# Statistics in larger pieces, a gather moved behind a projection, and a product moved between two others, in an attention and scan kernel

## The chip, the cores and the metric

The kernel runs on one core of a Trainium2 chip. The time is that of one launch on the device, in microseconds (us); the smaller the better. The core has five engines that run side by side, each with its own queue of instructions, worked off in order: TensorE (PE in the profile) multiplies matrices, VectorE (DVE), ScalarE (ACT) and GpSimd (POOL) work on rows of numbers in 128 partitions, and SyncE (SP) issues the DMA transfers between the chip's main memory and the on-chip memory. TensorE writes its results to PSUM, which has eight banks; a bank is 512 float32 numbers in each partition. Everything here is float32.

## The reference

The input x has two images of 256 x 256 positions with 128 channels. Two layers are computed, each added to its input.

```python
x = x + attention(_gn(x))      # layer 0
x = x + scan(_gn(x))           # layer 1
```

`_gn` is a group norm: the 128 channels fall into 32 groups of 4, and every group of an image is brought to mean 0 and variance 1 over all its 65,536 x 4 numbers. So a layer can begin with an image only when the statistics of that whole image are there.

The attention projects each position to q, k, v1, v2 (128 x 128 weights), takes for every position (i, l) the softmax over j of q[i, l] . k[l, j], averages v2 with it, multiplies with v1 and projects once more.

The scan layer is a state space model over the positions of an image in row order:

```python
xi, z = split(x @ in_proj_w.T)                  # 256 channels each
xi = silu(depthwise_conv_3x3(xi) + conv_b)
dts, Bs, Cs = split(x_proj_w @ xi)              # 8, 16 and 16 rows
delta = softplus(dt_w @ dts + dt_b)
h = exp(delta * A) * h + (delta * xi) * B       # step by step, 256 channels x 16 states
y = sum(h * C) + Ds * xi
y = layernorm(y) * ln_g + ln_b
out = (y * silu(z)) @ out_proj_w.T
```

## The kernel before

**Preparation and the first statistics.** Line 72 and the lines after it load weights and biases, all through the sync queue. Lines 150 to 157 bring `A_logs` into order with 32 tiny transfers. Lines 168 to 195 turn the weights with TensorE, and each of the nine convolution taps is multiplied into the input projection (VectorE, line 185), so that projection and convolution become nine matmuls. Behind them `piece_stats` (line 246) reads image 1 in NT = 16 pieces of 128 x 32 positions into six buffers and has VectorE take `bn_stats` of each of the 32 groups: 128 numbers (32 positions x 4 channels) in each partition, six numbers out. `group_stats` (line 204) then makes the scale `rs` and shift `sh` of every channel: 32 `bn_aggr` on VectorE, each over the six numbers of every piece; a matmul with a matrix of 1/128 (`ones_mean`) for the mean over partitions; small VectorE operations; two more matmuls that bring the group's values to its channels; and a power of -1/2 on GpSimd. This part has no order written out by hand; the framework places it by its own costs, in the order of the program where nothing else speaks.

**Attention** (lines 278 to 575). 256 calls of two columns each, in an order written out by hand for TensorE, ScalarE, VectorE and GpSimd. The statistics of image 2 for layer 0 (`image_load`, `image_stats`, lines 491 to 501) and those of both images for layer 1 (`column_stats`, line 483) are spread over the calls, six pieces a call. `gather` (line 486) is `group_stats` on them. Image 2's layer-1 gather is the very last thing, since the attention's last columns belong to it.

**The scan stage** (from line 577). Its buffers take over the memory of the attention's, and so its first loads wait until the attention's last user of that memory is done. An image has 64 steps of four rows (1024 positions); there are 128 steps. A step has 32 units: 8 groups of 32 channels by 4 groups of 4 states. For a unit `decay` (ScalarE, line 958) writes exp(delta A) into one of two PSUM buffers, `drive` (GpSimd, line 968) makes delta xi B for two units at a time, `scan` (VectorE, line 980) runs the recurrence, and `product` multiplies with C: on VectorE (line 995) for 21 units of a step, on GpSimd (lines 995 and 1004) for 11. `remember` (ScalarE, line 985) keeps the last state. `add_up` (TensorE, line 1027) sums four units' products; a product's buffer is free again when that is done.

Beside the units run three chains that feed them and finish them. `project(k)` (line 623) prepares step k: it loads rows (`load`), turns and normalises them (`turn`, `normalise`), and runs the convolution matmuls (`conv`), the gate's matmuls (`gate`), and those for B, C and delta (`states`, `size`). Each of these writes one PSUM bank, the pool `ps_p` with a single buffer, and ScalarE empties it before the next may be written. `finish_row` (line 813) takes a finished row: `turn` and `stats`, the layer norm (`scales`, `norm`), `back` (the transposes into `yd`, line 865), `gated` (VectorE, line 873: yd times silu(z)), `mix` and `leave`. Its bank is `ps_f`, also a single buffer.

The order is written out by hand again, in slots: slot t holds unit t, and `at(t, piece)` puts a piece of the chains into slot t. `project(k)` begins 72 slots ahead of its step, so slots -84 to -1 hold nothing but the projections of steps 0, 1 and 2. A row's `gated` lies in the slots with t mod 8 = 5, so in units 5, 13, 21 and 29 of a step. In a slot the loop at line 1054 emits, for each engine in this order: fetch, drive, GpSimd's products, decay of unit t + 1, `scan(t)`, `product(t)`, the pieces that `at` put there, first those that aren't TensorE's, then TensorE's, `add_up`, and `remember(t)`:

```python
            if 0 <= t < end:
                scan(t)
                if not pooled(t):
                    product(t)
            others, on_pe = slots.pop(t, ((), ()))
            for piece, args in others:
                piece(*args)
```

Of the kernel before, what the change touches and what calls it, by code (L numbers as in the profile page):

```python
# [8 lines left out]
F32 = mybir.dt.float32  # L9
# [12 lines left out]
def attn_then_ssm_kernel(  # L22
# [46 lines left out]
    def column(name, src):  # L69

        t = const.tile([P, 1], F32, name=name)
        nc.sync.dma_start(out=t, in_=src.rearrange("(p o) -> p o", o=1))
        return t
# [9 lines left out]
    ones_mean = const0.tile([P, P], F32, name="ones_mean")  # L83
    nc.vector.memset(ones_mean, 1.0 / P)
# [4 lines left out]


# [9 lines left out]
    bq_c = column("bq_c", bq)  # L100
    bv1_c = column("bv1_c", bv1)
# [102 lines left out]
    def group_stats(stats, pool, psum, name, tag="mm"):  # L204


        mv = pool.tile([P, G, 2], F32, name="mv")
        for g in range(G):
            nc.vector.bn_aggr(mv[:, g, :], stats[:, g, :, :])
        gm_ps = psum.tile([P, G], F32, name="gm_ps", tag=tag)  # L210
        nc.tensor.matmul(gm_ps, ones_mean, mv[:, :, 0], start=True, stop=True)
        gm = pool.tile([P, G], F32, name="gm")
        nc.vector.tensor_copy(gm, gm_ps)
        dev = pool.tile([P, G], F32, name="dev")
        nc.vector.tensor_tensor(dev, mv[:, :, 0], gm, ALU.subtract)
        dev2 = pool.tile([P, G], F32, name="dev2")
        nc.vector.tensor_tensor(dev2, dev, dev, ALU.mult)
        pv = pool.tile([P, G], F32, name="pv")
        nc.vector.tensor_tensor(pv, dev2, mv[:, :, 1], ALU.add)
        ex = pool.tile([P, 2, G, CG], F32, name="ex")  # L220
        nc.vector.tensor_copy(ex[:, 0], gm.unsqueeze(2).to_broadcast([P, G, CG]))
        nc.vector.tensor_copy(ex[:, 1], pv.unsqueeze(2).to_broadcast([P, G, CG]))
        cs_ps = psum.tile([P, 2], F32, name="cs_ps", tag=tag)
        for i in range(2):
            nc.tensor.matmul(
                cs_ps[:, i : i + 1],
                ex[:, i].rearrange("p g c -> p (g c)"),
                ones_mean[:, 0:1],
                start=True,
                stop=True,  # L230
            )
        cs = pool.tile([P, 2], F32, name="cs")
        nc.vector.tensor_copy(cs, cs_ps)
        ve = pool.tile([P, 1], F32, name="ve")
        nc.vector.tensor_scalar(ve, cs[:, 1:2], GN_EPS, None, ALU.add)
        rs = const.tile([P, 1], F32, name=f"rs_{name}")
        nc.gpsimd.tensor_tensor(rs, ve, neg_half[:, 0:1], ALU.pow)
        sh = const.tile([P, 1], F32, name=f"sh_{name}")
        nc.vector.tensor_scalar(sh, cs[:, 0:1], rs, -1.0, ALU.mult, ALU.mult)
        return rs, sh  # L240

    gn0 = {}
    TT = 32
    NT = L // (P * TT)

    def piece_stats(b, k, stats, pool):

        xt = pool.tile([P, TT, C], F32, name="xt")
        nc.sync.dma_start(
            out=xt,  # L250
            in_=x_tok[b, k * P * TT : (k + 1) * P * TT, :].rearrange("(p t) c -> p t c", p=P),
        )
        for g in range(G):
            nc.vector.bn_stats(stats[:, g, k, :], xt[:, :, g * CG : (g + 1) * CG])

    with tc.tile_pool(name="st", bufs=1) as stp, tc.tile_pool(
        name="st_x", bufs=6
    ) as stx, tc.tile_pool(name="st_ps", bufs=2, space=PSUM) as st_ps:
        stats = stp.tile([P, G, NT, 6], F32, name="stats")
        for k in range(NT):  # L260
            piece_stats(0, k, stats, stx)
        gn0[0] = group_stats(stats, stp, st_ps, "0_0")

# [13 lines left out]
    gn1 = {}  # L277
    with ExitStack() as actx:
# [207 lines left out]
        def gather(to, b, stats, layer):  # L486
            to[b] = group_stats(stats, ap1, ps, f"{layer}_{b}", "t0")
# [119 lines left out]
    slots = {}  # L607

# [13 lines left out]

    def project(k):
# [6 lines left out]
        o = {}  # L630

# [24 lines left out]
        def turn(src, r, m):  # L656
            t_ps = o["t"] = ps_p.tile([P, RB, W], F32, name="t_ps", tag="p")
            for i in range(m):
                for t in range(WT):
                    nc.tensor.transpose(  # L660
                        t_ps[:, i, t * P : (t + 1) * P], o[src][:, r + i, t, :], ident
                    )
# [10 lines left out]
        def conv(h, i, taps):  # L673
            if taps[0] == 0:
                o["u"] = ps_p.tile([P, RB, W], F32, name="u_ps", tag="p")
# [26 lines left out]
        def gate(h, i):  # L702
            o["z"] = ps_p.tile([P, RB, W], F32, name="z_ps", tag="p")
# [21 lines left out]
        def states(i):  # L725
            o["xd_ps"] = ps_p.tile([64, TB], F32, name="xd_ps", tag="p")
# [17 lines left out]
        def size(h, i):  # L744
            o["dt"] = ps_p.tile([P, TB], F32, name="dt_ps", tag="p")
# [67 lines left out]
    def finish_row(k, b, row, t0, a):  # L813
# [84 lines left out]
        for i, piece in (  # L898
# [5 lines left out]
            (5, gated),  # L904
# [3 lines left out]
            at(a + i, piece, pe=piece in (turn, back, mix))  # L908

# [41 lines left out]
    def pooled(t):  # L951
        return t % NU - t % 2 in POOLED or t % NU == SINGLE
# [100 lines left out]
    with tc.manual_schedule(engines=engines):  # L1053
        for t in range(min(slots), max(slots) + 1):
# [14 lines left out]
            if 0 <= t < end:  # L1069
                scan(t)  # L1070
                if not pooled(t):
                    product(t)
# [50 lines left out]
```

## Time and profile before

| | us |
|---|---|
| time, median of 3 runs (15882.23 to 15885.26) | 15883.89 |
| the profiled execution's own time | 15886.66 |
| its span, first to last instruction | 15884.8 |
| `bn_stats` of image 1 begin | 41.55 |
| `sh` of image 1, layer 0, begins | 158.81 |
| last `bn_aggr` group of the attention begins | 2523.20 |
| first scan begins | 2675.52 |

Busy over the whole span: VectorE 14454.8 us (91%), TensorE 13780.9 (87%), GpSimd 13328.8 (84%), ScalarE 10796.7 (68%). The rows of the profile name an instruction by line, engine, operation, and tiles as output<-inputs, with sizes as partitions x elements; x16 is a count. In a timeline a row is the start, the duration, and then in brackets how long the engine had been idle and what ended that. In a table of groups a row has the busy time and the mean duration in ns, and behind the bar the idle time before such instructions and what ended most of it. PEclk, or the column behind GpSimd's in a table of stretches, is the clock that TensorE was granted, 1.00 being full. Neighbouring VectorE instructions can overlap by some ns in these records.

### The profile page before, as it was taken

The page shows a single profiled execution, that of the slowest core. Times are in us where ns is not written, and L with a number is a line of the kernel's source. Part 1 is how long each engine was busy: PE and PEld are TensorE (multiplying, and loading weights), DVE is VectorE, ACT ScalarE, POOL GpSimd, SP SyncE. Part 2 cuts the span into 40 slices and gives each one's busy share as a digit, 9 for nine tenths or more (in the row PEclk, how much of TensorE's full clock was granted, in tenths as well). Part 3 has the DMA queues.
Part 4 walks back from the last instruction along what each step waited for, and adds up shares of the span by engine and source line. Part 5 has one row for each costly group of instructions (what it writes and reads, how often), then busy time and mean ns, then how long its engine had stood idle before and what let it go on. Part 6 is the DMA issues. An engine that isn't in the chain of part 4 may idle for free. (4 is left out here: it accounts for less than half of the span.)

```text
span 15884.8 us, 178043 instructions
## 1 busy us (share of the span) xinstructions
PE 13780.9 (87%) x59451; PEld 7002.8 (44%) x59451; DVE 14454.8 (91%) x12356; ACT 10796.7 (68%) x20003; POOL 13328.8 (84%) x3344
## 2 busy tenths in 40 slices
PE   6999998888888888888888888888888888888886
PEld 4877884333333333333333333333333333333333
DVE  7665555999999999999999999999999999999998
ACT  3555554777777777777777677777777777777775
POOL 1111113999999999999999999999999999999998
PEclk8999998999999999999999999999999999999998
DMA  4322222767677767677777667777677767776675
GB/s 188 123 101 86 80 96 105 239 238 245 240 241 242 246 240 240 240 245 241 243 242 244 230 241 242 242 244 244 240 241 241 245 241 243 242 244 240 240 243 185
DMA packets 1428908, 3452.13 MB, mean 217 GB/s; under 512 B 119785, under 2 KB 711185, under 8 KB 1407505
## 3 DMA queue, kind: packets, MB, share of 16 engines
q1 hardware_dynamic: 1427984, 3440.73, 62.6%
q8 instruction: 468, 7.67, 0.2%
q14 instruction: 456, 3.73, 0.1%
HBM read 2752.41 MB, written 687.88 MB: 217 GB/s over the span
## 5 line engine op out<-in xcount | busy, mean ns | idle before, releaser
L968 POOL TENSOR_TENSOR hb<-du_r,bb 128x2048 f32<-128x2048 f32 x2048 | 9243.5, 4545 | 82.3 <-DMA du_r<-du_d 15.7
L980 DVE TENSOR_TENSOR_SCAN da<-da,state,hb 128x1024 f32<-128x1024 f32 x2688 | 6300.4, 2344 | 137.9 <-ACT da L958 134.3
L958 ACT ACTIVATE da<-delta_r,a_neg 128x1024 f32<-128x1024 f32 x4096 | 4580.7, 1118 | 88.9 <-DMA delta_r<-delta_d 10.1
L678 PE MATMUL u_ps<-xn,w_tap 128*128 128x512 f32 x9216 | 4335.3, 612 | 91.3 <-ACT sz L715 73.2
L995 DVE TENSOR_TENSOR yc<-da,cc 128x1024 f32<-128x1024 f32 x2688 | 3291.8, 1225 | 235.9 <-PE y L1027 69.1
L980 DVE TENSOR_TENSOR_SCAN hb<-da,state,hb 128x1024 f32<-128x1024 f32 x1408 | 3233.4, 2334 | 61.5 <-ACT state L985 47.7
L1004 POOL TENSOR_TENSOR yc<-hb,cc 128x2048 f32<-128x2048 f32 x640 | 2909.0, 4545 | 101.0 <-ACT state L985 81.1
L678 PEld LDWEIGHTS u_ps<-xn,w_tap 128*128 128x128 f32 x9216 | 1713.7, 195 | 2453.6 <-issue 1837.9
L1027 PE MATMUL y<-yc,sel 128*32 128x512 f32 x16384 | 2323.6, 689 | 18.5 <-POOL yc L1004 18.1
L435 POOL TENSOR_TENSOR x1g<-xc,bo_all 128x512 f32<-128x512 f32 x256 | 316.0, 1276 | 1840.5 <-DVE stats L484 1839.6
L985 ACT COPY state<-da 128x1 f32<-128x1 f32 x2688 | 425.9, 158 | 1637.5 <-DVE yc L995 1630.1
L830 PE MATMUL yt<-centre,ys 128*128 128x256 f32 x4096 | 1030.9, 395 | 284.7 <-ACT ob L891 284.7
L1027 PEld LDWEIGHTS y<-yc,sel 128*32 128x32 f32 x16384 | 470.2, 121 | 1790.0 <-issue 1646.5
L704 PE MATMUL z_ps<-xn,w_z 128*128 128x512 f32 x1024 | 696.3, 768 | 547.0 <-ACT xn L665 307.3
L746 PE MATMUL dt_ps<-xd,w_dt 8*128 8x512 f32 x1024 | 740.6, 811 | 482.0 <-ACT delta L757 385.6
L385 ACT ACTIVATE e<-s_ps,nmx 128x256 f32<-128x256 f32 x1024 | 477.6, 476 | 967.7 <-DVE nmx L376 960.0
L985 ACT COPY state<-hb 128x1 f32<-128x1 f32 x1408 | 268.5, 191 | 1242.7 <-DVE hb L980 1242.6
L830 PEld LDWEIGHTS yt<-centre,ys 128*128 128x128 f32 x4096 | 742.0, 191 | 464.4 <-ACT ob L891 381.9
L881 PE MATMUL o_ps<-w_out,szr 128*128 128x128 f32 x4096 | 793.9, 276 | 0.0
L881 PE MATMUL o_ps<-w_out,yg 128*128 128x128 f32 x4096 | 792.8, 275 | 0.0
L352 DVE TENSOR_TENSOR v<-v_ps,bv_all 128x512 f32<-128x512 f32 x256 | 177.1, 692 | 592.1 <-PE v_ps L345 592.1
L775 POOL TENSOR_TENSOR xs<-delta,xs 128x1024 f32<-128x1024 f32 x256 | 606.7, 2370 | 99.1 <-ACT delta L765 99.1
(134 smaller groups left out, 17280.7 us busy)
## 6 DMA issues: line engine op xcount, KB each, us to landing
bb<-bc_d SPq DMA_DIRECT2D x1024, 512.0 KB, 4.0
cc<-bc_d SPq DMA_DIRECT2D x1024, 512.0 KB, 5.3
delta_r<-delta_d SPq DMA_DIRECT2D x1024, 512.0 KB, 6.3
du_r<-du_d SPq DMA_DIRECT2D x1024, 512.0 KB, 5.2
sz_d<-sz SPq DMA_DIRECT2D x128, 1024.0 KB, 6.5
szr<-sz_d SPq DMA_DIRECT2D x512, 256.0 KB, 4.1
xs_d<-xs SPq DMA_DIRECT2D x128, 1024.0 KB, 9.5
xr<-xs_d SPq DMA_DIRECT2D x256, 512.0 KB, 5.9
```

Of the source, the lines that this page charges most:

```text
L678: nc.tensor.matmul(o["u"], w_tap[:, h, tap, :], xn[:, i * RB + dy : i * RB + dy + RB, dx : dx + W], start=(tap == 0), stop=(tap == 8),)
L704: nc.tensor.matmul(o["z"], w_z[:, h, :], xn[:, 1 + i * RB : 1 + (i + 1) * RB, 1 : W + 1], start=True, stop=True,)
L746: nc.tensor.matmul(o["dt"], w_dt[:, h, :], o["xd"][0:DR, i * TB : (i + 1) * TB], start=True, stop=True,)
L830: nc.tensor.matmul(o["yt"][:, j, :], ys[k, h][:, t0 + j * P : t0 + (j + 1) * P], centre[:, (1 - h) * P : (1 - h) * P + DI], start=(h == 0) ...
L881: nc.tensor.matmul(o["o"][:, j, :], o[by][:, h, j * P : (j + 1) * P], w_out[:, i, h, :], start=False, stop=(j == WT - 1 and h == NH - 1 an ...
L958: nc.scalar.activation(da, spreads["delta", k, h, q], AF.Exp, scale=a_neg[:, g, m : m + 1])
L968: nc.gpsimd.tensor_tensor(hb, spreads["pair", k, h, q], repeats["bb", k, h, m].unsqueeze(1).to_broadcast([P, 2, T]), ALU.mult,)
L980: nc.vector.tensor_tensor_scan(u["h"], u["da"], u["hb"], st, ALU.mult, ALU.add)
L985: nc.scalar.copy(st, units[t]["h"][:, T - 1 : T])
L995: eng.tensor_tensor(u["yc"], u["h"], repeats["cc", k, h, m], ALU.mult)
L1004: nc.gpsimd.tensor_tensor(yc, hb, repeats["cc", k, h, m].unsqueeze(1).to_broadcast([P, 2, T]), ALU.mult)
L1027: nc.tensor.matmul(y[q * CQ : (q + 1) * CQ, cols], sel, units[t + q]["yc"][:, cols], start=False, stop=(m == NSG - 1),)
```

## The change

- Image 1's layer-0 statistics are taken in 8 pieces of 128 x 64 positions in place of 16 of 128 x 32. A piece comes in two transfers of the old size, into three buffers in place of six; there are 256 `bn_stats` of 256 numbers, and each `bn_aggr` reads 8 x 6 numbers. The first two pieces, with their transfers, are put ahead of the weights in the program; the other six stay behind the preparation.
- `group_stats` is cut in two: `group_means` (the 32 `bn_aggr`) and `group_scales`, which gives two pieces, `means` and `scales`. The matrix `ones_mean` goes; the matmuls use columns of `centre`, which hold -1/256, and the copies out of PSUM become multiplications with -2. The small tiles become slices of one.
- For image 2 and layer 1 the attention's end runs `group_means` only. `means` goes into slot -2 of the scan stage and `scales` into slot -1.
- In `project(0)`, and there alone, the tiles go to the banks of `ps_f` and `ps_p` in turn.
- `gated` is emitted between `scan(t)` and `product(t)` of its slot, no longer behind the product. The slots are the same.
- Some small constants move from one pool to another.

```diff
+    TT0 = 2 * TT
+    NT0 = NT // 2
+    def piece_stats(b, k, stats, pool):
+        xt = pool.tile([P, TT0, C], F32, name="xt")
+        src = x_tok[b, k * P * TT0 : (k + 1) * P * TT0, :].rearrange("(p t) c -> p t c", p=P)
+        for t in range(0, TT0, TT):
+            nc.sync.dma_start(out=xt[:, t : t + TT], in_=src[:, t : t + TT])
+        for g in range(G):
+            nc.vector.bn_stats(stats[:, g, k, :], xt[:, :, g * CG : (g + 1) * CG])
+    first = ExitStack()
+    stp = first.enter_context(tc.tile_pool(name="st", bufs=1))
+    stx = first.enter_context(tc.tile_pool(name="st_x", bufs=3))
+    stats = stp.tile([P, G, NT0, 6], F32, name="stats")
+    for k in range(2):
+        piece_stats(0, k, stats, stx)
...
+    def group_means(stats, pool):
         mv = pool.tile([P, G, 2], F32, name="mv")
         for g in range(G):
             nc.vector.bn_aggr(mv[:, g, :], stats[:, g, :, :])
+        return mv
+    def group_scales(mv, pool, psum, name, tag="mm", work="gw"):
+        keep = const0 if name[0] == "0" else const
+        rs = keep.tile([P, 1], F32, name=f"rs_{name}")
+        sh = keep.tile([P, 1], F32, name=f"sh_{name}")
+        MEAN = -DI / P
+        o = {}
+        def means():
+            gm_ps = psum.tile([P, G], F32, name="gm_ps", tag=tag)
+            nc.tensor.matmul(gm_ps, centre[:, 0:P], mv[:, :, 0], start=True, stop=True)
+            w = o["w"] = pool.tile([P, 2, 2 * P], F32, name=work)
+            gm, dev, dev2, pv = (w[:, 1, i * G : (i + 1) * G] for i in range(4))
+            nc.vector.tensor_scalar(gm, gm_ps, MEAN, None, ALU.mult)
...
+            nc.vector.tensor_copy(ex[:, 1], pv.unsqueeze(2).to_broadcast([P, G, CG]))
+        def scales():
+            cs_ps = psum.tile([P, 2], F32, name="cs_ps", tag=tag)
+            for i in range(2):
+                nc.tensor.matmul(
+                    cs_ps[:, i : i + 1],
+                    o["ex"][:, i].rearrange("p g c -> p (g c)"),
+                    centre[:, 0:1],
+                    start=True,
+                    stop=True,
+                )
...
+            nc.gpsimd.tensor_tensor(rs, ve, neg_half[:, 0:1], ALU.pow)
+            nc.vector.tensor_scalar(sh, cs[:, 0:1], rs, -1.0, ALU.mult, ALU.mult)
+        return (rs, sh), (means, scales)
...
     with tc.tile_pool(name="st_ps", bufs=2, space=PSUM) as st_ps:
-        for k in range(NT):
+        for k in range(2, NT0):
             piece_stats(0, k, stats, stx)
         gn0[0] = group_stats(stats, stp, st_ps, "0_0")
+    first.close()
...
         def gather(to, b, stats, layer):
-            to[b] = group_stats(stats, ap1, ps, f"{layer}_{b}", "t0")
+            if (layer, b) == (1, B - 1):
+                last.append(group_means(stats, const))
+            else:
+                to[b] = group_stats(stats, ap1, ps, f"{layer}_{b}", "t0")
...
+    gn1[B - 1], pieces = group_scales(last[0], s1, ps_f, f"1_{B - 1}", "f", "yn")
+    for i, piece in enumerate(pieces):
+        at(i - 2, piece)
...
+        def bank(shape, name):
+            o["n"] = o.get("n", 0) + (k == 0)
+            pool, tag = ((ps_p, "p"), (ps_f, "f"))[o["n"] % 2]
+            return pool.tile(shape, F32, name=name, tag=tag)
...
-            t_ps = o["t"] = ps_p.tile([P, RB, W], F32, name="t_ps", tag="p")
+            t_ps = o["t"] = bank([P, RB, W], "t_ps")
...
             (4, back),
-            (5, gated),
             (7, mix),
             (8, leave),
         ):
             at(a + i, piece, pe=piece in (turn, back, mix))
+        between[a + 5] = gated
...
             if 0 <= t < end:
                 scan(t)
+            if t in between:
+                between[t]()
+            if 0 <= t < end:
                 if not pooled(t):
                     product(t)
```

The tiles `u_ps`, `z_ps`, `xd_ps` and `dt_ps` of `project` change to `bank` as `t_ps` does.

## The prediction

> **What bounds the kernel now.** I read the timeline of the first 160 us, the sync queue's waits there, the timeline round 2500 us, VectorE's groups in the scan stage, and single scan steps with the clock that TensorE was granted. Times are us from the span's start.
>
> ```profile
> 8.73 20.60 SPq L152 DMA_DIRECT2D alog_d<-in_L_conv_A_logs_dram  x32
> 32.41 71.57 SPq L249 DMA_DIRECT2D xt<-in_x_dram  x16
> 41.55 99.29 DVE L254 BATCH_NORM_STATS2 stats<-xt 128x6 f32<-128x128 f32 x512 [0.15 <-issue]
> 140.73 14.44 DVE L209 BATCH_NORM_AGGREGATE mv<-stats 128x2 f32<-128x96 f32 x32
> 158.81 0.21 DVE L239 TENSOR_SCALAR sh<-cs,rs 128x1 f32<-128x1 f32 x1 [0.73 <-POOL rs L237]
> ```
>
> Until 158.81 nothing but statistics ends late: the sync queue issues weights up to 32.41, 32 tiny transfers (0.64 each) among them; then VectorE alone works, 512 x 194 ns and 32 x 451 ns. The queue's waits:
>
> ```profile
> SPq L142 <- DMA bo_all<-in_L_conv_bo_dram: 0.2, 1, 0.2
> SPq L145 <- DMA cb_c<-in_L_conv_conv_b_dram: 0.2, 1, 0.2
> ```
>
> Each names the transfer eight places before it: no more than eight are under way.
>
> ```profile
> 2523.20 14.43 DVE L209 BATCH_NORM_AGGREGATE mv<-stats 128x2 f32<-128x96 f32 x32
> 2541.54 0.21 DVE L239 TENSOR_SCALAR sh<-cs,rs 128x1 f32<-128x1 f32 x1 [0.66 <-POOL rs L237]
> 2541.89 0.36 SPq L635 DMA_DIRECT2D raw<-x  x1
> ```
>
> ```profile
> 2669.83 9.86 PE L678 MATMUL u_ps<-xn,w_tap 128*128 128x512 f32 x18 [0.68 <-ACT sz L715]
> ...
> 2675.52 2.36 DVE L980 TENSOR_TENSOR_SCAN da<-da,state,hb 128x1024 f32<-128x1024 f32 x1 [133.76 <-ACT da L958]
> ```
>
> Image 2's gather lies bare (2523.20 to 2541.75), and only then may the scan stage load into the freed memory. From 2546.6 to 2675.52 TensorE and ScalarE take turns on one PSUM bank.
>
> ```profile
> L980 DVE TENSOR_TENSOR_SCAN da<-da,state,hb 128x1024 f32<-128x1024 f32 x2350 | 5508.1, 2344 | 3.8 <-POOL state L1059 3.3 <-ACT da L958 0.5
> L995 DVE TENSOR_TENSOR yc<-da,cc 128x1024 f32<-128x1024 f32 x2350 | 2877.8, 1225 | 205.3 <-PE y L1027 59.6 <-DVE da L980 1.4 <-issue 0.4
> L980 DVE TENSOR_TENSOR_SCAN hb<-da,state,hb 128x1024 f32<-128x1024 f32 x1230 | 2824.7, 2334 | 55.6 <-ACT state L985 42.0 <-ACT da L958 13.2 <-issue 0.2
> L873 DVE TENSOR_TENSOR yg<-yd,szr 128x512 f32<-128x512 f32 x447 | 304.3, 681 | 0.0
> ```
>
> From 2675.52 on VectorE is the bound: 11,515 us busy in a window of 11,500 (neighbours overlap). The idle time before L995 is partly a dependence: a product, which reads what the scan wrote, starts 34 ns or more after the scan's recorded end; independent neighbours start 83 ns before it. One step (32 units, from 5756.70 to 5859.11: 102.41) shows the rest. Windows (TensorE, weights, VectorE, ScalarE, GpSimd busy, then clock), then unit 13, then unit 28:
>
> ```profile
> 5796.82:5800.23 3.41, 3.41 (x11) 0.92 (x4) 3.32 (x3) 3.38 (x3) 3.33 (x3) 0.50 0.91 317
> 5800.23:5803.65 3.42, 3.42 (x13) 1.69 (x12) 3.39 (x3) 3.33 (x6) 3.42 (x1) 1.00 1.03 379
> 5844.61:5848.02 3.41, 3.21 (x10) 0.90 (x14) 3.41 (x2) 3.10 (x8) 3.41 (x2) 0.50 0.93 301
> 5848.02:5851.43 3.41, 3.41 (x17) 1.17 (x10) 3.10 (x3) 3.38 (x3) 3.41 (x2) 1.00 0.64 245
> ```
>
> ```profile
> 5799.62 2.35 DVE L980 TENSOR_TENSOR_SCAN da<-da,state,hb 128x1024 f32<-128x1024 f32 x1
> 5802.00 1.23 DVE L995 TENSOR_TENSOR yc<-da,cc 128x1024 f32<-128x1024 f32 x1
> 5803.14 0.68 DVE L873 TENSOR_TENSOR yg<-yd,szr 128x512 f32<-128x512 f32 x1
> 5803.74 4.58 DVE L980 TENSOR_TENSOR_SCAN hb<-da,state,hb 128x1024 f32<-128x1024 f32 x2
> ```
>
> ```profile
> 5801.91 0.60 PE L865 MATMUL yd<-ident,yn 128*128 128x128 f32 x4
> ```
>
> ```profile
> 5849.35 1.22 DVE L995 TENSOR_TENSOR yc<-da,cc 128x1024 f32<-128x1024 f32 x1 [0.31 <-PE y L1027]
> ```
>
> The clock is halved in stretches of 3.4, 6.8 or 10.2 us. Unit 28's product waits 0.31, of it 0.22 for TensorE's sums, which ran at half clock until 5848.02. Most steps take 102.40 to 102.46, 30 x 3.413.
>
> The Trainium skill ("TensorE: Matmul & The Clock Gate", "Part 1: The HAM clock gate") says that this gate judges activity in free-running windows of 3413 ns. The stretches agree; by the rule a step tied to the gate can only take whole windows, and a VectorE saving below one window would be worth nothing.
>
> **The change, part by part.**
>
> *First statistics.* Eight pieces of 64 tokens instead of sixteen of 32: 256 bn_stats of 256 elements. No row has that length; it costs between 194 ns (no growth) and 388 (double). VectorE's products of 1024 start the next instruction 1141 ns later, the gate products of 512 598: 1.06 ns an element and 54 fixed, which gives 190 at 128 (194 measured) and 326 at 256. I take 326: 10.4 a piece. bn_aggr reads 48 numbers instead of 96: between 225 and 451 ns; with the same fixed part 253, so 8.1 instead of 14.4.
>
> Four transfers of 2.1 MB now lead the queue. Before, the first such one landed 7.9 after its issue (40.31), the next 4.85 apart; from 0.73 on that is 8.6, 13.5, 18.3 and 23.2. The transfers in places 9 to 12 wait for these. The twelfth, lng_c, leaves at 23.2 instead of 4.10: all behind it moves by 19.1, the tiny transfers included, and the third piece leaves at 32.41 + 19.1 = 51.5 and has landed at 64.3. Weight preparation (32.0 to 41.5 before) ends at 60.6, hidden there. VectorE does pieces one and two meanwhile and stands idle; six pieces follow without a gap, since a piece lands in 9.7: 64.3 + 62.6 = 126.9, not 140.84. With 8.1 and the unchanged 3.8 of the scale chain, sh is there at 138.9 instead of 159.02. Late next: the attention's second load, issued behind the last bn_stats, lands 12.7 later (139.6) and costs about 0.9; the first statistics piece of image 2, queued behind it, lands at 144.5, and VectorE, in order, reaches v2 0.9 late. Front: 20.1 - 0.9 - 0.9 = 18.3 gained. Ends: 3 (bn_stats of pieces one and two queued behind the preparation) and 43 (the third piece's transfers ahead of the weights, VectorE never idle).
>
> *Image 2's gather.* The 32 bn_aggr stay; the chain behind them (2537.63 to 2541.75) leaves this place: loads start 4.1 earlier.
>
> *Two banks in the first projection.* TensorE's waits for the bank there were 0.70, 0.87, 0.96, three of 0.78 and four of 0.68 up to 2589.56: 7.6. Later ones, beside the second projection, were 0.67, 0.67 and four of 0.78: 4.5. At the border between the two (2598.33) ScalarE's copies keep 0.6 of 0.78. Sum 12.2, if every one goes. If the clock then stays full in the two convolutions that took 9.7 and 9.8 instead of 7.99, 3.5 more; taken as 0.
>
> *The moved chain.* It sits in slots -2 and -1, ahead of the first scan on VectorE, and its first matmul stands behind 16 of 18 matmuls of the third projection's first convolution: 2669.83 + 16/18 x 9.86 = 2678.6. From matmul to sh the chain took 4.0; with the last tap between, 4.3. GpSimd's pow queues behind one drive product, already done. The first scan would be at 2682.9; less 4.1 and 12.2, 2666.6 instead of 2675.52: 8.9 gained of 16.3. VectorE being the bound, it holds to the end.
>
> *Gate product inside* (four a step). Between scan and product it fills the dependence: 34 + 83 = 117 ns saved. In units 5 and 29 the transposes yd are done 3.3 and 0.24 before the new start. In unit 21 the gain is lost: the next scan waits 0.375 for ScalarE's decay anyway. In unit 13 yd ends at 5802.51, while the scan lets go at 5799.62 + 2.26 = 5801.88: VectorE waits 0.67, and the next scan starts 0.55 later than 5803.74. Its decays keep 0.6 us of slack or more. The product, which waited for nothing, now queues behind that wait.
>
> What settles it is the phase to the clock windows. After a late step the trace shows unit 28's wait falling 1.19, 0.71, 0.47, 0.35 with steps of 103.36, 102.89, 102.64, 102.52: the wait shrinks by half of any drift, until the step is 102.40. VectorE's saving of 3 x 0.117 = 0.35 must then reappear in unit 28: 0.22 + 0.35 = 0.57. At that phase yd comes early: in the steps with waits of 0.71 and 0.47 it ended 1.73 and 1.49 after scan 13's start, before 2.26. So unit 13 costs nothing, and neither is anything gained: 102.40 again. I take 0 for the 128 steps. The ends: 45 gained (128 x 0.35, no tie to the clock) and 49 lost.
>
> [...]
>
> Sum: 18.3 + 8.9 + 0 = 27.2. The profiled execution took 15886.66 (span 15884.8), 2.8 over the median of 15883.89; off the median, **15856.7**.
>
> **Rivals.**
> 1. *Slower: unit 13's wait becomes VectorE's limit.* Two steps with waits of 0.46 show yd at 3.13, where others of 0.47 have 1.49: there the wait jumps. With units shifted by 0.12 the jump is at 0.52; the tie holds if the gates save over 0.30 together. Below that each round passes the jump, some 6.5 steps a window instead of 16: (3.41/6.5 - 3.41/16) x 128 = 40 lost; without feedback (0.55 - 0.12 - 0.05) x 128 = 49. It decides from 27.2/128 = 0.21 a step. 15897 to 15906.
> 2. *The gates bring their time*, if the scan stage isn't tied: 45 more, 15812. Against: 102.40 to 102.46 in most steps.
> 3. *The front gains nothing*: VectorE holds the first pieces behind the preparation: 3 instead of 18, 15872. For it: the queue's order delays all weights.
>
> **Numbers.** Forecast 0.53, rivals 0.21, 0.08, 0.18. A measurement tells about 0.2% (31.8) from no change. The forecast's own range is 15840 to 15874 (bn_stats 0.30 to 0.36; 3.5 of clock; whole windows of 3.4), so 0.4 of it is beyond 0.2%: faster 0.21 + 0.08 + 0.02 from rival 3 = 0.31; slower 0.08 from rival 1 and 0.02 from others; same 0.59. Range: leaving out rival 2 and the upper end of rival 1, 15828 to 15902.
>
> **What would show it.** bn_stats of about 0.33 in two groups with a gap before 64; sh near 139; the first scan near 2648 (2675.5 - 18.3 - 8.9); steps of 102.4 with a wait near 0.57 at unit 28 and none before the gate product of unit 13. Wrong if steps average over 102.9 or under 102.4, or if the third piece lands far from 64.

## The result and the profile after

The changed kernel took 15842.3 us (median of nine runs, 15839.0 to 15846.1) against 15883.5: a ratio of 0.9974, interval 0.9966 to 0.9982, so 41 us gained where 27.2 were forecast. Its profiled execution has a span of 15840.8 against 15884.8, 44.0 less. All times below are us.

Where the 44.0 lie, read off at four marks of the two traces:

| mark | before | after | gained up to here | forecast |
|---|---|---|---|---|
| image 2's last bn_aggr begin | 2523.20 | 2505.61 | 17.6 | 18.3 |
| first scan | 2675.52 | 2638.52 | 37.0 | 27.2 |
| last scan ends | 15829.57 | 15786.43 | 43.1 | 27.2 |
| span | 15884.8 | 15840.8 | 44.0 | 27.2 |

The start, VectorE's timeline (start, duration, engine, line, operation, tiles; in brackets the idle time before it and what ended that):

```profile
13.21 21.03 DVE L103 BATCH_NORM_STATS2 stats<-xt 128x6 f32<-128x256 f32 x64 [11.29 <-DMA xt<-in_x_dram]
...
63.22 62.87 DVE L103 BATCH_NORM_STATS2 stats<-xt 128x6 f32<-128x256 f32 x192 [3.29 <-DMA xt<-in_x_dram]
126.01 7.48 DVE L230 BATCH_NORM_AGGREGATE mv<-stats 128x2 f32<-128x48 f32 x32
...
137.12 0.21 DVE L269 TENSOR_SCALAR sh<-gw,rs 128x1 f32<-128x1 f32 x1 [0.67 <-POOL rs L268]
```

192 bn_stats in 62.87 are 327 ns each (forecast 326); they end at 126.0 (126.9), bn_aggr takes 7.5 (8.1), sh is there at 137.3 (138.9). The sync queue shows what the third piece still waits for:

```profile
0.73 1.92 SPq L101 DMA_DIRECT2D xt<-in_x_dram  x4
...
27.14 20.60 SPq L173 DMA_DIRECT2D alog_d<-in_L_conv_A_logs_dram  x32
...
50.82 44.99 SPq L101 DMA_DIRECT2D xt<-in_x_dram  x12
```

Round 2500 the chain behind the 32 bn_aggr is gone from its old place, and TensorE starts at 2524.84 instead of 2546.63. Its timeline from there:

```profile
2525.29 2.02 PE L697 MATMUL t_ps<-ident,raw 128*128 128x128 f32 x8
2527.31 1.50 PE L741 MATMUL z_ps<-xn,w_z 128*128 128x512 f32 x2
2528.65 23.34 PE L715 MATMUL u_ps<-xn,w_tap 128*128 128x512 f32 x54
2551.83 2.93 PE L741 MATMUL z_ps<-xn,w_z 128*128 128x512 f32 x6
...
2626.13 9.31 PE L715 MATMUL u_ps<-xn,w_tap 128*128 128x512 f32 x16 [0.68 <-ACT sz L752]
2635.28 0.30 PE L244 MATMUL gm_ps<-mv,centre 128*128 128x32 f32 x2
```

In the first projection there is no wait left, and three convolutions take 23.34 in one run, where the first alone took 11.06 before. The matmul gm_ps of the moved chain stands behind 16 of the 18 matmuls, as forecast.

In the scan stage nearly every step still takes 102.40. A regular step shows the two places that the forecast was about, unit 13 and unit 28 (VectorE's timeline of step 23):

```profile
5039.04 2.35 DVE L1017 TENSOR_TENSOR_SCAN da<-da,state,hb 128x1024 f32<-128x1024 f32 x1
5041.30 0.67 DVE L910 TENSOR_TENSOR yg<-yd,szr 128x512 f32<-128x512 f32 x1
5041.89 1.21 DVE L1032 TENSOR_TENSOR yc<-da,cc 128x1024 f32<-128x1024 f32 x1
...
5089.05 1.22 DVE L1032 TENSOR_TENSOR yc<-da,cc 128x1024 f32<-128x1024 f32 x1 [0.72 <-PE y L1064]
```

Unit 13's gate product starts 2.26 after its scan, without a wait. What the gate products save reappears at unit 28: 0.72 of idle time, 0.31 before.

The exceptions are seven steps of 104.5, each followed by 103.2 and 102.65 to 102.8; before there were eight steps of 103.9 to 104.6. Each such train, a slip in what follows, adds up to one clock window (3.4) over steps of 102.40. One of them, step 24, at units 8, 13 and 28:

```profile
5124.93 2.33 DVE L1017 TENSOR_TENSOR_SCAN da<-da,state,hb 128x1024 f32<-128x1024 f32 x1
5127.70 1.23 DVE L1032 TENSOR_TENSOR yc<-da,cc 128x1024 f32<-128x1024 f32 x1 [0.44 <-DVE da L1017]
...
5144.89 0.69 DVE L910 TENSOR_TENSOR yg<-yd,szr 128x512 f32<-128x512 f32 x1 [0.75 <-PE yd L902]
...
5193.38 1.23 DVE L1032 TENSOR_TENSOR yc<-da,cc 128x1024 f32<-128x1024 f32 x1 [1.45 <-PE y L1064]
```

Unit 8's product starts 0.44 after the scan whose data it reads, where 0.09 is usual. It waits for no other engine. This stall of 0.352 delays a product once in 16 steps, in the kernel before too (there at units 12 and 18), and it had no place in the forecast. Much of what follows is about it. Six of the seven slips begin with it, and seven of the eight before. The remaining slip of each begins elsewhere: ScalarE waits for the transfer that brings `delta_r`, here in step 14 of the kernel before and in step 39 of the changed one; no run shows why it lands late just there.

```profile
4121.02 1.12 ACT L958 ACTIVATE da<-delta_r,a_neg 128x1024 f32<-128x1024 f32 x1 [1.74 <-DMA delta_r<-delta_d]
...
6647.29 1.12 ACT L995 ACTIVATE da<-delta_r,a_neg 128x1024 f32<-128x1024 f32 x1 [1.26 <-DMA delta_r<-delta_d]
```

### The profile page after: what moved, and what is told of

It reads as the page before. It is cut to its first block, busy times and chain, and to the rows that moved or that the text cites. A ratio compares the mean times of both kernels' runs of the same rounds, so it can differ in the third digit from the quotient of the medians.

```text
span 15840.8 us, 177783 instructions
## 1 busy us (share of the span) xinstructions
PE 13760.4 (87%) x59451; PEld 6981.7 (44%) x59451; DVE 14380.1 (91%) x12099; ACT 10833.2 (68%) x20003; POOL 13334.4 (84%) x3344
## 5 line engine op out<-in xcount | busy, mean ns | idle before, releaser
L715 PE MATMUL u_ps<-xn,w_tap 128*128 128x512 f32 x9216 | 4239.5, 601 | 37.1 <-ACT sz L752 33.4
L1032 DVE TENSOR_TENSOR yc<-da,cc 128x1024 f32<-128x1024 f32 x2688 | 3285.2, 1222 | 255.7 <-PE y L1064 104.9
L715 PEld LDWEIGHTS u_ps<-xn,w_tap 128*128 128x128 f32 x9216 | 1675.0, 191 | 2326.8 <-issue 1873.3
L1064 PE MATMUL y<-yc,sel 128*32 128x512 f32 x16384 | 2415.4, 713 | 18.5 <-POOL yc L1041 17.7
L741 PE MATMUL z_ps<-xn,w_z 128*128 128x512 f32 x1024 | 738.4, 812 | 626.4 <-ACT xn L702 313.8
L783 PE MATMUL dt_ps<-xd,w_dt 8*128 8x512 f32 x1024 | 696.8, 766 | 507.1 <-ACT delta L794 415.1
L918 PEld LDWEIGHTS o_ps<-w_out,yg 128*128 128x128 f32 x4096 | 664.9, 193 | 27.1
```

The costliest lines, as they stand in the source:

```text
L715: nc.tensor.matmul(o["u"], w_tap[:, h, tap, :], xn[:, i * RB + dy : i * RB + dy + RB, dx : dx + W], start=(tap == 0), stop=(tap == 8),)
L741: nc.tensor.matmul(o["z"], w_z[:, h, :], xn[:, 1 + i * RB : 1 + (i + 1) * RB, 1 : W + 1], start=True, stop=True,)
L783: nc.tensor.matmul(o["dt"], w_dt[:, h, :], o["xd"][0:DR, i * TB : (i + 1) * TB], start=True, stop=True,)
L918: nc.tensor.matmul(o["o"][:, j, :], o[by][:, h, j * P : (j + 1) * P], w_out[:, i, h, :], start=False, stop=(j == WT - 1 and h == NH - 1 an ...
L1032: eng.tensor_tensor(u["yc"], u["h"], repeats["cc", k, h, m], ALU.mult)
L1064: nc.tensor.matmul(y[q * CQ : (q + 1) * CQ, cols], sel, units[t + q]["yc"][:, cols], start=False, stop=(m == NSG - 1),)
```

## The experiments

Each was timed beside the kernel before, whose median was 15885 to 15888 in these comparisons; gains against it are taken within each. Gains against the changed kernel are taken against its 15842.3, and carry those 3 us or so. First one part of the change at a time.

**Gate products alone.** On the kernel before:

```diff
             if 0 <= t < end:
                 scan(t)
+            if t in between:
+                between[t]()
+            if 0 <= t < end:
                 if not pooled(t):
                     product(t)
```

> The kernel before with the gate product issued between a unit's scan and its product, and nothing else. Theory (tie): the 0.35 us a step that VectorE saves come back as a longer wait of unit 28's product (0.31 of idle before it becomes about 0.7), steps stay at 102.4, and the time stays within 7 us of 15883.5, that is 15877 to 15887, with a step or two more or less of 3.4 us. Rival 1 (gates bring their time): 128 x 0.35 = 45 less, 15838, steps of 102.05. Rival 2 (unit 13's gate product waits 0.67 in every step and is the limit): 40 to 49 more, 15923 to 15932.

15857.0, 29.5 less than 15886.5 (ratio 0.9983, 0.9974 to 0.9992): none of the three. The tie itself held: the median step is 102.40 and unit 28's idle time 0.71. What went is the slips: one of eight is left, and that one (step 94) begins with `delta_r`, 1.10 late, not with a stall. The stall is still there, in the same steps and at the same units 12 and 18. Step 37, first of the kernel before (TensorE's sums, then the products of units 12 and 28), then the same two products with the gate products alone:

```profile
6511.52 3.64 PE L1027 MATMUL y<-yc,sel 128*32 128x512 f32 x16
...
6515.65 1.23 DVE L995 TENSOR_TENSOR yc<-da,cc 128x1024 f32<-128x1024 f32 x1 [0.46 <-PE y L1027]
...
6567.66 1.23 DVE L995 TENSOR_TENSOR yc<-da,cc 128x1024 f32<-128x1024 f32 x1 [1.45 <-PE y L1027]
```

```profile
6502.90 1.23 DVE L996 TENSOR_TENSOR yc<-da,cc 128x1024 f32<-128x1024 f32 x1 [0.44 <-issue]
...
6553.87 1.22 DVE L996 TENSOR_TENSOR yc<-da,cc 128x1024 f32<-128x1024 f32 x1 [0.55 <-PE y L1028]
```

The first product's row names TensorE, but the sums end at 6515.16, half a microsecond before it starts. With 0.31 of spare time at unit 28 a stall of 0.35 made the sums so late that the step lost a window; with 0.71 it only shortens the wait to 0.55. So here the gate products bring no shorter step, but a margin.

**Larger pieces alone.** The changed kernel with its other three parts undone, cut to the lines that put them back:

```diff
-            pool, tag = ((ps_p, "p"), (ps_f, "f"))[o["n"] % 2]
+            pool, tag = (ps_p, "p")
...
-            if (layer, b) == (1, B - 1):
-                last.append(group_means(stats, const))
-            else:
-                to[b] = group_stats(stats, ap1, ps, f"{layer}_{b}", "t0")
+            to[b] = group_stats(stats, ap1, ps, f"{layer}_{b}", "t0")
...
+            (5, gated),
...
-        between[a + 5] = gated
```

> The changed kernel with the gate products, the banks and the second image's gather put back as before: the first statistics in larger pieces are what is left of the change. The prediction's term was 18.3, the trace of the changed kernel has 17.6 at the start of image 2's last bn_aggr (2523.20 against 2505.61): 15883.5 - 17.6 = 15866, give or take one clock window of 3.4. Rival (the attention stage hides part of it, as the prediction's third rival had it): 3 less, 15880.

15852.7, 33.8 less (0.9981, 0.9972 to 0.9990). Up to image 2's bn_aggr 18.0 are gained, as read from the traces, and 1.7 more on the way to the first scan; but the scan stage is 14.2 shorter too (13139.8 against 13154.1), though nothing in it was edited. There are four slips instead of eight: the stall now falls on unit 0 in the first image (three times, a slip each time; the fourth slip begins with a late `delta_r`) and on unit 20 in the second. At unit 20 it costs nothing: in that step the wait of 0.375 at unit 22, for ScalarE, is gone instead.

**Two banks alone.** On the kernel before, the function `bank` of the change, used for all tiles of the projections.

> The kernel before with the first projection's tiles alternating between the two PSUM banks, and nothing else. The prediction's term was 12.2, the bank waits alone: 15871. Rival, read from the trace of the changed kernel: from TensorE's first transpose to the third projection's first convolution it took 101.3 instead of 123.2, 21.9 less: 15862, with the convolutions of the first projection at 7.8 each instead of 11.1, 8.0, 8.0 and 8.0, since the clock stays full and the matmuls' own latency no longer lies between them.

15866.2, 20.4 less (0.9988, 0.9979 to 0.9997). In the trace the first scan is at 2652.63, 22.9 earlier, of which 1.1 is already there at TensorE's first transpose: 21.8, the rival's reading. The scan stage takes exactly as long as before, 13154.05 in both.

The three alone sum to 83.7, and the change with all three brings 41. The parts are at odds somewhere, and most of it lies in the scan stage: gates and pieces alone shorten it by 29.5 and 14.2, the whole change by 6.1. A smaller rest lies ahead of it: the first scan comes 2.8, 19.7 and 22.9 earlier in the three, 45.3 in sum, and 37.0 with the whole change. The gather moved behind the projection is in that 37.0, and was not run alone.

**Where the stall falls.** Counting VectorE's instructions in the traces, those that only handle semaphores included, every stall that I saw sits at a number that leaves 63 when divided by 128: 6079, 7487, 8895 and 10303 in the kernel before, 6847 and 12095 with the larger pieces alone. A step has 88 instructions, and 16 steps are 11 times 128. The reverse does not hold. Of the eleven such numbers in 16 steps of the kernel before (first image) three show the stall: the product of unit 12 and two semaphore instructions, at units 3 and 23, which start 0.35 late within a wait that ends no later for it. At the other eight nothing starts late. The change leaves VectorE 253 instructions fewer, all ahead of the scans, and that shifts the stall. So five idle instructions more, and nothing else:

```diff
     nc.vector.memset(neg_half, -0.5)
+    spare = const.tile([P, 1], F32, name="spare")
+    for _ in range(5):
+        nc.vector.memset(spare, 0.0)
```

> The changed kernel with five more VectorE instructions (memsets of 128x1, 0.06 us each) at the very start, where VectorE waits 11 us for data anyway; nothing else. Theory (place of the stall): VectorE stalls 0.352 us once in 16 steps, always at an instruction whose number in its stream, semaphore instructions counted, leaves 63 when divided by 128; a step is 88 instructions, so the stall's place in the step repeats every 16 steps and depends on the number of instructions ahead, modulo 8. Before and the kernel with the gates alone have 253 more instructions ahead than the changed kernel; 253 is 5 modulo 8. With five more the stall moves from units 8 and 0 (where it made unit 13 wait 0.75 and cost a clock window of 3.4 us each time) to units 12 and 18 (where unit 28's spare 0.6 takes it up, as in the kernel with the gates alone): six or seven slips fewer, 20 to 25 less than 15842, 15817 to 15824. Rival (the slips have another cause, and five idle memsets do nothing): 15842 give or take 4.

15816.7 (0.9958, 0.9945 to 0.9970): 25.7 less than the changed kernel, by five instructions that do nothing. The stall sits at units 12 and 18, and none of the seven slips is left. Units 12 and 28 of step 34:

```profile
6159.00 1.23 DVE L1035 TENSOR_TENSOR yc<-da,cc 128x1024 f32<-128x1024 f32 x1 [0.44 <-issue]
...
6209.97 1.23 DVE L1035 TENSOR_TENSOR yc<-da,cc 128x1024 f32<-128x1024 f32 x1 [0.57 <-PE y L1067]
```

**Why units 8 and 0 are bad places.** By the trace of step 24 the stall delays what TensorE does next so that unit 13's transposes come late, which the gate product inside now waits for. TensorE in step 23, without a stall, and in step 24; below, the table of stretches for the matmuls ahead of the transposes (busy time of TensorE, weights, VectorE, ScalarE and GpSimd, then the clock):

```profile
5037.35 2.84 PE L715 MATMUL u_ps<-xn,w_tap 128*128 128x512 f32 x6
5040.03 0.60 PE L902 MATMUL yd<-ident,yn 128*128 128x128 f32 x4
...
5140.45 3.96 PE L715 MATMUL u_ps<-xn,w_tap 128*128 128x512 f32 x6
5144.25 0.60 PE L902 MATMUL yd<-ident,yn 128*128 128x128 f32 x4
```

```profile
5037.00:5040.00 3.00, 3.00 (x10) 1.19 (x7) 2.91 (x3) 2.97 (x3) 2.92 (x2) 1.00 0.95 296
5140.00:5144.00 4.00, 4.00 (x10) 1.70 (x7) 3.91 (x3) 3.97 (x3) 3.92 (x2) 0.66 1.04 296
```

The half clock lasts 6.83 in step 23 and ends at 5036.93; in step 24 it lasts one window more, 10.24, and ends only at 5142.74. So a stall of 0.35 makes the transposes 1.83 later, counted from the step's start. The first attempt to take that wait away was a misreading:

> The changed kernel with one order changed on TensorE: in slot 12 of a step the four transposes yd, which unit 13's gate product needs, are issued ahead of three matmuls of a convolution instead of behind them, so yd is ready 1.3 to 2.5 us earlier. Theory: the stall at units 8 and 0 stays where it is, but unit 13 no longer turns it into a wait of 0.75, unit 28's spare time takes it up, and the slips of 3.4 us go: 20 to 25 less than the changed kernel, 15817 to 15824, steps still 102.40. Rival (unit 13 plays no part, the late sums alone cause the slips): 15842 give or take 4.

15843.6 (0.9973), the changed kernel's time. The edit changed nothing in TensorE's order: a tap of an f32 convolution is two matmul instructions, so the six that stood ahead of the transposes were the three taps of slot 11, not of slot 12. The run is a repetition of the changed kernel. The right edit issues the transposes a slot earlier:

```diff
+            i -= piece is back and a % NU == 8
             at(a + i, piece, pe=piece in (turn, back, mix))
```

> The changed kernel with the four transposes yd of the row whose gate product sits in unit 13 issued one slot earlier on TensorE, so ahead of the six matmuls of the convolution that they stood behind (the run labelled yd_first left that order as it was and so repeated the changed kernel). yd is then ready about 3 us earlier, at every phase to the clock windows before unit 13 asks for it. Theory: the stall of 0.35 us stays at units 8 and 0, unit 13 no longer turns it into a wait of 0.75, unit 28's spare 0.6 takes it up, and the six or seven slips of 3.4 us go: 20 to 25 less than 15842, 15817 to 15824, steps still 102.40. Rival (the slip comes from the late sums and units 22 and 28 alone): 15842 give or take 4.

15815.3 (0.9956, 0.9944 to 0.9969), 27.0 less than the changed kernel. The stall has not moved; units 8, 13 and 28 of step 24:

```profile
5124.98 1.23 DVE L1033 TENSOR_TENSOR yc<-da,cc 128x1024 f32<-128x1024 f32 x1 [0.44 <-DVE da L1018]
...
5141.32 0.67 DVE L910 TENSOR_TENSOR yg<-yd,szr 128x512 f32<-128x512 f32 x1
...
5188.91 1.22 DVE L1033 TENSOR_TENSOR yc<-da,cc 128x1024 f32<-128x1024 f32 x1 [0.55 <-PE y L1065]
```

Unit 13 no longer waits, unit 28 takes the stall up, and no slip is left. That shows both halves of the cause: stall ahead of unit 13, and gate product that waits for late transposes. Taking away either one is worth about 26 us. Some 20 of them are the six slips of the stall; the seventh, which began with `delta_r` 1.26 late, may be missing by luck, since no `delta_r` is later than 1.06 and 0.76 in the traces of these two runs.

**The tie itself.** Unit 28 waits for the sums of units 20 to 23, which stand on TensorE behind z, and z behind ScalarE. Issued ahead of z:

```diff
+            early = t % NU == 26
+            if early and 0 <= t - 6 < end:
+                add_up(t - 6)
             for piece, args in on_pe:
                 piece(*args)
...
-            if 0 <= t - 6 < end and (t - 6) % NQ == 0:
+            if not early and 0 <= t - 6 < end and (t - 6) % NQ == 0:
                 add_up(t - 6)
```

> The changed kernel with one piece moved: in slot 26 of a step the sums y of units 20 to 23 are issued on TensorE ahead of the z matmul, which waits 2.5 us for ScalarE, instead of behind it. Theory (tie): unit 28's product no longer waits for sums that run at half clock after z; the idle time before it falls from 0.72 to under 0.1, the step leaves the multiple of the clock window (102.40) for 101.75 to 101.95, and the slips of 3.4 us every 16 steps end too: 128 x 0.5 to 0.65 + 20 = 84 to 103 less than the changed kernel, 15740 to 15760. Rival (something else holds the step at 102.4: ScalarE's decays, GpSimd at 99%): within 8 us of 15842. Second rival: z, now behind the sums, is 1 us later, the convolution and the transposes yd of unit 13 or 29 with it, and a wait there takes half of the gain: 15790 to 15810.

15818.4 (0.9958, 0.9946 to 0.9971), 24 less than the changed kernel: the slips went, the tie stayed. Unit 28 does not wait any more, but steps settle at 102.40 again, now at unit 13 (step 20):

```profile
4724.41 2.35 DVE L1017 TENSOR_TENSOR_SCAN da<-da,state,hb 128x1024 f32<-128x1024 f32 x1
4727.29 0.69 DVE L910 TENSOR_TENSOR yg<-yd,szr 128x512 f32<-128x512 f32 x1 [0.53 <-PE yd L902]
```

So the theory of one waiting place was too narrow: the next wait for TensorE takes over, at another phase to the windows. The run meant to free both used the same mistaken edit as above and repeats this one:

> The changed kernel with both orders changed on TensorE: the sums of units 20 to 23 ahead of z in slot 26, and the transposes yd ahead of the convolution's taps in slot 12. With the first alone the steps still took 102.39: unit 13's gate product had become the place that waits (0.54 in most steps). Theory (any wait for TensorE whose length depends on the clock ties the step to whole windows; without one it is free): neither unit 28 nor unit 13 waits, the step is VectorE's own, about 102.40 - 0.53 = 101.87, no multiple of 3.413, and the stall costs its 0.35 only: 0.5 x 127 + some 10 for lost windows = 65 to 80 under the 15818 of the sums alone, 15740 to 15755. Rival: the next wait for TensorE (unit 12's product, for the sums of slot 10) ties it again at 102.40: within 15 of 15818. Second rival: GpSimd, which idles only 0.8 us a step, holds it at 101.6 to 102: 15735 to 15770 with waits before scans for hb.

15818.7 (0.9959). With the transposes really earlier:

> The changed kernel with the sums of units 20 to 23 ahead of z in slot 26, and the transposes yd of unit 13 one slot earlier, ahead of the convolution. With the first alone (15818) unit 13's gate product waited 0.54 and held the step at 102.40. Theory (only a wait for TensorE at half clock ties the step to whole windows): now neither unit 28 nor unit 13 waits, the step is VectorE's own with ScalarE's 0.4 at unit 22, about 102.40 - 0.53 = 101.87, no multiple of 3.413; the phase drifts through all values and unit 12's product waits at some of them: 15745 to 15775. Rival: unit 12's wait for the sums of slot 10 ties it at 102.40 again: 15803 to 15825. Second rival: GpSimd, idle 0.8 us a step, holds it between 101.9 and 102.2: 15765 to 15800.

15792.8 (0.9940, 0.9926 to 0.9953), 49.5 less than the changed kernel. The tie is broken: the median step is 102.01, no multiple of 3.413, and most steps lie between 101.76 and 102.06. The expected 15745 to 15775 were missed, since unit 12 now waits for TensorE, over 0.3 in 21 of 111 steps. Step 45, with ScalarE early in the step, then unit 12:

```profile
7240.82 1.12 ACT L996 ACTIVATE da<-delta_r,a_neg 128x1024 f32<-128x1024 f32 x1 [0.81 <-DMA delta_r<-delta_d]
...
7271.87 2.33 DVE L1018 TENSOR_TENSOR_SCAN da<-da,state,hb 128x1024 f32<-128x1024 f32 x1
7275.27 1.22 DVE L1033 TENSOR_TENSOR yc<-da,cc 128x1024 f32<-128x1024 f32 x1 [1.07 <-PE y L1065]
```

The drifting phase alone does not explain these waits. In each of the 21 steps ScalarE had waited 0.47 or more for `delta_r`; in the 36 steps where it waited under 0.3 there are none. Late transfers are not enough either, as 34 steps with 0.6 and more show no wait at unit 12. ScalarE waits over 0.3 for `delta_r` in 8 of these 111 steps of the changed kernel and in 75 here, so with the tie gone this transfer comes next; no run moved it. The average step is 102.21 (steps 5 to 121, without the six round the change of image); unit 12's idle time averages 0.25 in it.

**What the gate products are worth without the tie.** The same kernel with them behind the unit's product again:

```diff
+            (5, gated),
...
-        between[a + 5] = gated
```

> The kernel whose step had come loose from the clock windows (sums ahead of z, transposes yd one slot earlier; 15792.8, steps of 102.01 in the median and 102.21 on average), with its gate products put back behind the unit's product as before the change: what the gate products inside are worth where nothing ties the step. Theory (they save 117 ns each in units 5, 13 and 29 and nothing in unit 21, and VectorE alone sets the step there): 0.35 x 127 = 45 more, 15838, with a longest bound of four savings, 15852. Rival (ScalarE's decays at units 22 and 30 and GpSimd, idle 0.8 us a step, hold the step, and the product's order is worth nothing): within 10 of 15793. Second rival (without the gates the step comes to 102.4 by itself and is caught by the windows again): 102.40 x 127, about 15818 to 15830.

15818.0 (0.9956, 0.9943 to 0.9969): 25 for the gate products (22 if each is taken against the kernel before in its own comparison). The second rival's time is met, but not its reason: the steps are 102.19 and 102.28, not caught at 102.40. The average step is 102.395 without and 102.212 with the gate products, 0.18 apart. Four times 117 ns are 0.47; of it 0.10 goes into a longer wait at unit 22 (0.386 to 0.484 on average), 0.10 into one at unit 30 for ScalarE that was not there, and 0.08 into unit 12 (0.171 to 0.251): 0.19 is left.

**The tiny transfers.** On the changed kernel, the 32 transfers of A_logs moved behind the last statistics piece (with the load and the two operations on their result):

```diff
         for k in range(2, NT0):
             piece_stats(0, k, stats, stx)
+        alog_d = dram.tile([CQ, SR, NCG, NSG], F32, name="alog_d")
+        for g in range(NCG):
+            for m in range(NSG):
+                nc.sync.dma_start(
...
         gn0[0] = group_stats(stats, stp, st_ps, "0_0")
```

> The changed kernel with the 32 tiny transfers of A_logs (20.6 us of the sync queue from 27.14 to 47.74), the load of their result and the two operations on it issued behind the last statistics piece instead of among the weights. Theory (the third piece leaves late because of the sync queue's issues alone): it leaves at 30.2 instead of 50.8, the bn_stats end at about 105 instead of 126, sh comes at 117 instead of 137.3, the scan stage is as before: 15842 - 20 = 15822, give or take a clock window. Rival (the tiny transfers now delay the attention's first loads or compete with the pieces): 10 or more of it is lost, 15832 or more.

15826.3 (0.9963, 0.9951 to 0.9976), 16 less than the changed kernel. The pieces do what was expected, and five of the 21 are lost behind them. The sync queue of that run:

```profile
29.56 44.84 SPq L101 DMA_DIRECT2D xt<-in_x_dram  x12
74.44 33.11 SPq L273 DMA_DIRECT2D alog_d<-in_L_conv_A_logs_dram  x32
107.67 0.51 SPq L316 DMA_DIRECT2D xc<-in_x_dram  x1
```

The third piece leaves at 29.56 and the bn_stats end at 104.9; but the tiny transfers, which took 20.6 among the weights, take 33.1 among the pieces, and hold the attention's first load until 107.67. VectorE's first `v` of the attention comes 12.4 after sh instead of 7.9.

**Together.** The three edits that helped, on the changed kernel:

> The changed kernel with the three edits that helped: sums of units 20 to 23 ahead of z, transposes yd of unit 13 one slot earlier, and the 32 tiny transfers of A_logs behind the last statistics piece. The gains lie in different stages and add: 15792.8 less the 16 that the late transfers brought to the changed kernel, 15777, give or take 5. Rival (the start of the scan stage at another phase costs windows): up to 7 more.

15778.4 (0.9932, 0.9918 to 0.9946): 64 less than the changed kernel and 109.5 less than before in the same comparison. The expected 15777 is met by the median, but the five runs fall into two groups, three at 15776 to 15778 and two at 15788 to 15790. So how much of the 16 adds to the 15792.8 is not firm.

## Why the prediction was right, and where it was not

The time lies in the range and in the forecast's own range (15840 to 15874), 14 under the number. By the prediction's own line of 0.2% (31.8) the 41 are a faster kernel, for which it had 0.31, and 0.59 for no difference. That it came so near is in part luck: two terms were off, by 9.7 in the banks and by a balance in the scan stage that was not foreseen. By its steps:

- *First statistics*, 18.3: measured 17.6, and 18.0 alone. The fixed part of 54 ns and 1.06 ns an element held for 256 elements (327 against 326), and the eight places of the queue put the third piece where it was forecast (63.2 against 64.3). The loss behind sh was larger than the 1.8 assumed: 21.7 gained at sh, 17.6 at the end of the attention.
- *Gather chain*, 4.1: TensorE's start follows the bn_aggr by 19.23 instead of 23.43, so 4.2.
- *Two banks*, 12.2: measured 21.9 (from the first transpose to the third projection's first convolution 101.29 instead of 123.20). This term is the one that was mis-sized most. The waits were summed rightly: TensorE's idle time between these two marks falls from 22.9 to 10.1, 12.8 less, 8.4 of it in the first projection. What was "taken as 0" was not: convolutions at half clock gave back 3.1 in the first projection and 2.5 in the second, 5.6 against the 3.5 named and dropped. The remaining 3.5 were not taken apart. Other matmuls got shorter too (the first two z matmuls took 2.05 and take 1.50), and with no wait between them the next matmuls start before the modelled end of the last.
- *Moved chain*, 7.4 lost: from that convolution to the first scan it took 12.39 instead of 5.69, 6.7. So the fill gained 4.2 + 21.9 - 6.7 = 19.4 and not 8.9.
- *Gate products*, 0 in steps of 102.40: steps stayed at 102.40 and unit 28's idle time rose by 0.41, forecast 0.35. The tie to the clock windows is what these runs show, down to its breaking when neither unit 28 nor unit 13 has to wait. The Trainium skill ("TensorE: Matmul & The Clock Gate", "Part 1: The HAM clock gate") gives the window as 3413 ns; the half clock of 6.83 and 10.24 in steps 23 and 24 is two and three of them. But the 0 of the sum was right by a balance that the prediction did not know. It treated the late steps of before as given. Seven of the eight come from VectorE's stall of 0.352 every 16 steps, and there the two parts meet: the gate products' margin would have removed these slips (29.5 alone), and the larger pieces moved the stall ahead of unit 13, where the gate product inside turns it into a wait of 0.75 and brings the slips back. Left over were 6.1, of them 3.4 for one slip fewer and 2.0 in the last three steps.
- *Rival 1* (unit 13's wait) was right in its mechanism and wrong in its extent: the wait came, 0.75, but in seven steps, not in all, since the steady phase has room for yd. It costs these seven windows, some 24 us. *Rival 2* (45 gained) comes out at 22 to 30 by either way that was measured, as margin with the tie and as shorter steps without. *Rival 3* did not happen.

Open: what makes VectorE stall at some of these places and not at others. The profile of the changed kernel lists 453 packets of 8 KB and 467 of 16 KB on its instruction queues, 1387 times 8 KB in all, and the trace has 177,783 instructions, 1389 times 128. So one 8 KB for every 128 instructions fits, and the stall may be the loading of instructions; no run shows it. Why a stall at unit 12 or 18 needs more than 0.31 of spare time at unit 28, while only 0.16 of it is then used, was not followed up either.

## What to carry to other kernels

Before pricing a saving in a steady loop, look for a wait whose length depends on a quantised resource, here TensorE's clock: the saving then becomes margin there, and pays only through the rare steps that overrun it, until every such wait on the critical engine has been taken away. When single edits sum to more than they bring together, compare the stage lengths of the single runs: the conflict lies in the stage that none of them seemed to touch. And when a pipe with one buffer gets a second, add the clock that comes back and the overlap of neighbours to the waits.

## What the runs showed of the hardware that was not expected

- VectorE stalled 0.352 at some of the instructions whose number in its stream leaves 63 modulo 128, among them, once in 16 steps, a product that would otherwise start 0.09 after the scan; five idle instructions ahead moved it from units 8 and 0 to units 12 and 18 and were worth 25.7 us.
- One stall of 0.35 cost 3.4, a whole clock window, spread over some six steps, where a wait for half-clocked TensorE had less room than it needed (unit 28 in the kernel before, unit 13 in the changed one). So did a transfer of `delta_r` that ScalarE had to wait for by 1.1 to 1.8.
- The same 32 tiny transfers held the sync queue for 20.6 among other small transfers and for 33.1 beside transfers of 2.1 MB.
